# A planned decoder layer on one core: other buffers for the end of the last batch, the true length of one fp32 matmul in the planner, and new dates

## The chip, the core and the metric

The kernel runs on one core of a Trainium2 chip. A core has five engines that run side by side, each through its own instructions in order: TensorE (PE, matrix products into the accumulators in PSUM), VectorE (DVE), ScalarE (ACT), GpSimd (POOL) and SyncE (SP, which here issues nearly all DMA transfers). They wait for each other by semaphores alone. The metric is the device time of one execution in microseconds (us). Before the change the runs took 1061.47, 1062.81 and 1063.2 us (median 1062.81).

## The reference

One decoder layer over 8 batches of 512 rows of width 256, in fp32, with a layer norm after each of three parts:

```python
# 1: linear attention in chunks of 32 rows, gated
S = einsum('bncd,bnkd->bnck', Qc, Kc) * mask        # decay ** distance, causal
out = sigmoid(x @ W_g.T) * (S @ V) @ W_o.T + x
x = layernorm(x + out)
# 2: cross-attention, 16 heads of 64, over 512 context rows
qw, kw, vw = x @ Wq + bq, ctx @ Wk + bk, ctx @ Wv + bv
a = softmax(where(key_mask, qw @ kw.T / 8, -inf))
x = layernorm(x + (a @ vw) @ Wo + bo)
# 3: FFN with ternary weights, hidden size 1024, and a path of rank 16
h = bitlinear(x, w_fc) + gate * (x @ v.T @ fast_b.T @ u.T)
x = layernorm(x + bitlinear(relu(h) ** 2, w_proj))
```

`bitlinear` rounds a weight row to -1, 0 or 1 by its mean magnitude and scales it with that mean.

## The kernel before

**Arithmetic.** Nearly every fp32 product is made of two fp16 parts, a high one and a low one (`x - high`), and of three products of them (`PASSES`). So wherever a matrix is made, ACT (or POOL) writes the high part and DVE or POOL the low one. The ternary weights need no low part.

**Units.** Batch after batch, the cross-attention goes over 8 pairs of heads, and for each pair over 4 blocks of 128 query rows: 256 units in all, `(b, p, qt)`. One unit is: 6 score matmuls of 64 by 512 on PE, two heads side by side on the two halves of the array (`scores`, tile `s`); for each head a row maximum on DVE that also adds the mask (`tensor_tensor_reduce`, in the trace CUSTOM_DVE and a read of the accumulator, tile `nm`); for each head an exponential on ACT (tile `e`); the high part of the probabilities on ACT or POOL and the low part on DVE (`split_p`, tile `ph`); a DMA transpose of two units together on SP's queue (`pT` from `ph`, in the last two head pairs one unit at a time, the very last by PE); and 24 small matmuls of 64 columns (`attend`, tile `av`) some six units later. After four units of a pair the division, the split and a transpose give `oT` (through `of` and `oh`; in the last two pairs after two units, through `ofl` and `ohl`, with PE transposes).

**Between the units** stand the other stages, cut into pieces: k, v, q of head pairs to come (tiles `pk`, `pvv`, `pq`, `W`), the linear attention of the next batch (`gen_l0`), and the output projection (`pwo`) and FFN (`ph`, `r`, `rh`, `py`, `y`) of the batch before. In batch 0 the weights are prepared there too (`setup_wo`, `setup_ffn`). After the last unit there is a written tail: the rest of the projection of batch 7 (`wo_tail`, tile `pwl`) and its FFN in two halves of 256 rows (`ffn_tail`: `pz`, `r4`, `rhl`, `pyl`, `yl`), row blocks one at a time.

**The planner sets the order.** The body of the kernel only records operations. Each carries a date, `nc.prio`: the number of the unit at which it is recorded, plus an offset by its kind (`LATE`; `TP` in the tail). How early a piece of a stage is recorded is set by the budget that is pulled from its queue at each unit (`PULL`: "k" for k, q and v, "l" for the next batch's first part, "w" for the weights, "f" for projection and FFN, "g" the same in batch 7). `schedule` then runs a model of the engines, with a length for each operation from `cost`, and at each moment starts on every free engine the ready operation of the earliest date; `REACH` says how much later a date it may take in place of an earlier one that would collide with POOL. What comes out is one fixed order for each engine. All instructions are emitted from one line, 451, so the profile tells them apart by tile names.

**Buffers are part of the plan.** A tile with a tag takes a slot of a ring; most rings are served in the order in which the program recorded the tiles (`in_order`), and a tile that has no slot holds back its operation in the plan. The rings that matter here: `tmp2` (4 slots of 2 KB: `of`, `r4`, `y`, and before the change `ofl`, `ohl`, `yl`), `t4` (5 slots: `rh`, and before the change `rhl`), `pT` and `ph` (3 slots each, probabilities), `x1T` and `ctxh` (2 each: the inputs of q and of k and v).

**The fp32 matmul.** One product is left in fp32: in `setup_ffn`, `ones` times `dg` spreads the scale of the second FFN weight over all partitions (tile `ps2`, shown as `ps`), and DVE copies it to `s2b`. `cost` gave every matmul `n / 2400 + 0.0025` us for n columns.

Of the kernel before, what the change touches and what calls it, by code (L numbers as in the profile page):

```python
# [11 lines left out]
F16 = mybir.dt.float16  # L12
F32 = mybir.dt.float32
# [5 lines left out]
B, T, D = 8, 512, 256  # L19
H, DH = 16, 64  # L20
# [6 lines left out]
LAG = 4  # L27
BURST = 2
MARGIN = 0.0
REACH = 9.52  # L30
SPARE = 1
DLATE = 1.6
PTS = 3
PHS = 3
NWP = 4
TP = (0.35, 0.96, 1.15, 3.0, 0.5, 5.1)
STICK = 2.09
HOLD = 0.18
HIGH = ("apaa", "paaa", "papp")
LATE = {"k": 0.0, "q": 0.0, "v": 0.53, "w": -0.33, "l": -0.41, "o": -0.91, "f": 0.31, "s": 0.0, "a": 0.91, "t": 0.0, "x": 0.31, "e": 0.0, "c": -1.28, "d": -0.95}  # L40
PULL = {"k": 5.13, "l": 2.62, "w": 3.61, "f": 4.71, "g": 5.48}

PASSES = ((0, 0), (0, 1), (1, 0))

# [109 lines left out]
class Recorder:  # L154
# [34 lines left out]
    def add(self, engine, method, args, kw):  # L189
# [9 lines left out]
        if engine in ("DVE", "ACT") and method[:3] != "dma" and self.prio >= 0:  # L199
            src = ins[0].t if ins else None  # L200
            if method == "tensor_tensor_reduce":
                o.prio += LATE["t"]
            elif method == "activation" and args[2] == AF.Exp:
                o.prio += LATE["x"]
            elif src is not None and src.pool[:2] == "ps":
# [45 lines left out]
    def cost(self, o, ins, outs):  # L251

        n = max([int(np.prod(x.shape[1:])) for x in outs + ins] or [0]) if o.engine != "PE" else outs[0].idx.size
        psum = any(x.t.pool[:2] == "ps" for x in ins + outs)
        ones = sum(x.idx.size == 1 and x.t.free > 0 for x in ins)
        o.half, o.port = None, o.engine == "POOL"
        o.dma = o.method[:3] == "dma"
        if o.dma:
            x = (outs or ins)[0]
            if o.method == "dma_start_transpose":  # L260
                blocks = n / 128
                o.occ, o.lat = 0.1 * blocks + 0.4, 0.115 * blocks + 0.55
            else:
                size = {F32: 4, F16: 2}.get(x.t.dt, 1)
                o.occ, o.lat = 0.45, n * size * x.shape[0] / (380e3 if self.prio < 0 else 210e3) + (1.2 if size == 1 else 0.1)
        elif o.engine == "PE":
            o.occ = n / 2400 + 0.0025
            o.lat = o.occ + 0.17
            if ins[0].p1 - ins[0].p0 == 64:
                o.half = ins[0].p0  # L270
        elif o.engine == "DVE":
            lat = 0.145 + n * 1.042e-3
            if o.method == "tensor_tensor_reduce":
                o.occ, o.lat = 0.615, 0.8
                return
            if not psum and o.method in ("tensor_copy", "tensor_scalar") and n >= 512:
                lat = 0.12 + n * 0.62e-3
            if psum and ones and o.method == "scalar_tensor_tensor":
                lat += 0.065
            if n <= 8:  # L280
                lat = 0.19 if o.method == "reciprocal" else 0.175 if o.method == "bn_aggr" else 0.145
            o.occ, o.lat = lat - 0.085, lat
            o.port = not psum and o.method in ("tensor_tensor", "scalar_tensor_tensor", "tensor_scalar", "tensor_copy")
        elif o.engine == "ACT":
            lat = 0.165 + n * 0.83e-3 + (0.0 if psum else 0.04) + 0.07 * ones
            o.occ, o.lat = (lat + 0.01, lat + 0.12) if "accum_out" in o.kw else (lat - 0.11, lat)
        elif o.engine == "POOL":
            if o.method == "tensor_tensor":
                lat = 0.3 + n * 1.67e-3 if n <= 512 else 0.2 + n * 1.9e-3
                if o.args[3] == ALU.pow:  # L290
                    lat = 0.42 + 0.16 * n
            else:
                lat = 0.13 + n * 0.9e-3 if n > 512 else 0.92 if n == 256 and o.kw == {} and o.method == "tensor_scalar" and o.args[-1] == ALU.is_lt else 0.62 if n > 256 else 0.56 if n > 8 else 0.22 + n * 5e-3
            o.occ, o.lat = lat - 0.03, lat


    def schedule(self):
# [37 lines left out]
        while done < len(ops):  # L335
# [10 lines left out]
            while again:  # L346
                again = False
                for e in engines:
# [22 lines left out]
                    while e != "PE" and avail[e]:  # L371
                        x = heapq.heappop(avail[e])
                        if pick is not None and x[0] > pick[0] + REACH:
                            aside.append(x)
# [98 lines left out]
def decoder_kernel(ctx: ExitStack, tc: tile.TileContext, ins: dict, out: bass.AP):  # L473
# [4 lines left out]
    wk = ctx.enter_context(Pool(nc, "wk", 1))  # L478
# [5 lines left out]
    def t4(name, shape, dt=F16):  # L484
        return wk.tile(shape, dt, tag="t4", name=name, bufs=5)

    def tmp2(name, shape, dt=F32):
        return wk.tile(shape, dt, tag="tmp2", name=name, bufs=4)
# [252 lines left out]
    rows, x1T, x2T, ctxh, mb, oT = {}, {}, {}, {}, {}, {}  # L741
# [288 lines left out]
    def ffn_tail(b, i, base, step_):  # L1030
        row = rows[b]
        rh, py = {}, {}
        ts = slice(256 * i, 256 * i + 256)
        PL = 3
        for s_ in range(8 + PL):
            nc.prio = base + step_ * s_
            if s_ == 0:
                zst = ffn_z(b, ts, f"{b}_{i}", ("zst", "sph")[i])
            if s_ < 8:
                j = s_  # L1040
                r4 = ffn_h(b, j, ts, zst, f"{b}_{i}", True)
                hl = t4(f"rhl{i}{j}", [128, 2, 256])
                if i == 0 or j % 2:
                    nc.scalar.activation(r4, r4, AF.Square)
                else:
                    nc.vector.tensor_tensor(r4, r4, r4, ALU.mult)
                if j % 2:
                    nc.scalar.copy(hl[:, 0], r4)
                else:
                    nc.vector.tensor_copy(hl[:, 0], r4)  # L1050
                (nc.vector if j % 3 == 2 or (i == 1 and j == 7) else nc.gpsimd).tensor_tensor(hl[:, 1], r4, hl[:, 0], ALU.subtract)
                rh[j] = hl
            if s_ >= PL:
                j = s_ - PL
                if j == 0:
                    for t in range(2):
                        py[t] = misc(f"pyl{i}{t}")[:, :D]
                hl = rh.pop(j)
                for t in range(2):
                    for a in range(2):  # L1060
                        nc.tensor.matmul(py[t], hl[:, a, t * 128:(t + 1) * 128], tpj[:, j, :],
                                         start=(j == 0 and a == 0), stop=(j == 7 and a == 1))
            yield
        for t in range(2):
            tt = 2 * i + t
            y = tmp2(f"yl{tt}", [128, D])
            nc.vector.tensor_tensor(y, py[t], s2b, ALU.mult)
            nc.vector.tensor_tensor(row[:, tt], row[:, tt], y, ALU.add)
            layernorm(b, row, EPS, "c", tt, 1, True)
            nc.sync.dma_start(out[b, tt * 128:(tt + 1) * 128], row[:, tt, :])  # L1070
        yield


    pT, av, den = {}, {}, {}
# [58 lines left out]
    def attend(u):  # L1133
        b, p, qt = u
# [3 lines left out]
        o, v, t = av[b, p][:, qt], vp[b, p], pT.pop(u)  # L1138
# [7 lines left out]
        if tail:  # L1146
            if qt == 0:
                oT[b, p] = wk.tile([128, 2, T], F16, tag="oT", name=f"oT{b}_{p}", bufs=8)
            if qt % 2:
                d = den[b, p][:, qt - 1:qt + 1, :]  # L1150
                nc.vector.reciprocal(d, d)
                of = tmp2(f"ofl{p}{qt}", [128, 2, 2, DH])
                nc.vector.scalar_tensor_tensor(of, av[b, p][:, qt - 1:qt + 1], sc, d.unsqueeze(3).broadcast_to([128, 2, 2, DH]), ALU.mult, ALU.mult)
                oh = tmp2(f"ohl{p}{qt}", [128, 2, 2, 128], F16)
                ofv = of.rearrange("p t h n -> p t (h n)")
                nc.scalar.copy(oh[:, 0], ofv)
                nc.vector.tensor_tensor(oh[:, 1], ofv, oh[:, 0], ALU.subtract)
                dst = oT[b, p][:, :, (qt - 1) * 128:(qt + 1) * 128].rearrange("p a (t n) -> p a t n", t=2)
                for a in range(2):
                    pe_T(dst[:, a], [oh[:, a, t_] for t_ in range(2)], f"o{p}{qt}{a}", a)  # L1160
            return
        if qt == 3:
            d = den.pop((b, p)).rearrange("p t h -> p (t h)")
            nc.vector.reciprocal(d, d)
            of = tmp2(f"of{b}_{p}", [128, 4, 128])
# [3 lines left out]
            oh = wk.tile([128, 2, 4, 128], F16, tag="oh", name=f"oh{b}_{p}", bufs=1)  # L1169
# [62 lines left out]
    for p in range(2):  # L1232
        g = gen_kv(0, p)
# [13 lines left out]
    def at(i, off):  # L1247
        now[0], nc.prio = i, i + off
# [18 lines left out]
    for i, u in enumerate(units):  # L1267
        b, p, qt = u
# [26 lines left out]
        f = 1 + (0.5 - p % 2) * 0.2  # L1295
# [18 lines left out]
    U = len(units)  # L1314
# [18 lines left out]
            if pend:  # L1333
                attend(pend.pop(0))

    at(U, 1)
    bf.drain()
    at(U, TP[0])
    rest(len(pend) - 4)
    wo_tail(0)  # L1340
    f0, f1 = ffn_tail(b, 0, U + TP[1], TP[2]), ffn_tail(b, 1, U + TP[3], TP[4])
    go(f0, 3)
# [10 lines left out]
    go(f0, 1)  # L1353
    at(U, TP[5])
    ffn_end(b - 1)
# [47 lines left out]
```

## Time and profile before

The profiled execution took 1061.94 us; its span, from the first to the last instruction, is 1060.1 us.

| | busy us | share of the span |
|---|---|---|
| PE matmul | 998.2 | 94% |
| DVE | 986.9 | 93% |
| ACT | 879.4 | 83% |
| POOL | 544.8 | 51% |
| packets of SP's queue | | 95.6% of 16 DMA engines |

The largest groups: exponentials (512 of 705 ns on ACT), row maxima (512 of 710 ns on DVE), low parts of the probabilities (256 of 1298 ns on DVE), `av` (6144 matmuls), scores (1536 matmuls), and 131 transposes of `ph` on SP's queue, 7.5 us from issue to landing in the median.

How to read it: start times are us from the span's start. The first unit's row maximum starts at 45.4, that of batch 1 at 168.1, of batch 2 at 284.4, of batch 7 at 898.3; the middle batches take 122 to 123 us each. In a timeline a row gives start, length, engine, line, operation, tiles and shapes, and how many instructions it merges; in square brackets stands the idle time of the engine before it and what ended that. In the table of stretches each engine has its busy time and, after x, its instructions; PEclk is the mean TensorE clock that was granted, 1.00 being full. The share of a busy engine is no proof that it is the bound: a row can hold time in which the instruction only waited for a port or a pipeline.

### The profile page before, as it was taken

To read this page: it belongs to the slowest core of one execution; us is meant where nothing else is said; L and a number is where in the kernel's file an instruction comes from. 1 tells how busy PE (TensorE), PEld (TensorE's weight loads), DVE (VectorE), ACT (ScalarE), POOL (GpSimd) and SP (SyncE) were. 2 spreads that over 40 slices of the span, in tenths; PEclk is the share of its full clock that TensorE was granted. 3 is DMA by queue.
4 is the path that set the end of the run, shared out by engine and by line. 5 is a ranking of instruction groups with operands and counts; after the bars stand their busy time and mean duration, and the time that the engine had idled before them with its cause. 6 is when DMAs were issued, how large, how long until landed. Compare 5 with 4: busy or idle time off the path is not lost.

```text
span 1060.1 us, 29949 instructions
## 1 busy us (share of the span) xinstructions
PE 998.2 (94%) x11976; PEld 639.3 (60%) x11976; DVE 986.9 (93%) x2101; ACT 879.4 (83%) x1876; POOL 544.8 (51%) x513
## 2 busy tenths in 40 slices
PE   7986889999999999999999999999999999999986
PEld 4644545665666656665666656766567656665664
DVE  7999989999999989999899989999899998998976
ACT  7787778889977998789977898879977889878836
POOL 0251282256841596245861577426962548443635
PEclk9999989999999999999999999999999999999989
DMA  8289799999999999989999999999999999999861
GB/s 306 99 147 186 133 214 186 164 180 191 186 185 189 174 179 168 207 155 189 185 184 204 162 185 179 192 189 156 195 163 214 154 185 170 187 167 201 138 115 41
DMA packets 646636, 185.65 MB, mean 175 GB/s; under 512 B 628448, under 2 KB 641376, under 8 KB 646496
## 3 DMA queue, kind: packets, MB, share of 16 engines
q1 hardware_dynamic: 645632, 183.42, 95.6%
q8 instruction: 93, 1.52, 0.6%
q10 hardware_dynamic: 864, 0.32, 0.1%
q14 instruction: 47, 0.39, 0.1%
HBM read 21.18 MB, written 4.19 MB: 24 GB/s over the span
## 4 chain that ended last, share of the span: by engine, by line
PE 41%; ACT 17%; DVE 17%; DMA 12%; issue 6%; POOL 4%; SPq 2%; ACTq 0%; POOLq 0%; DVEq 0%
PE av L451 8%; PE s L451 8%; DMA pT<-ph 6%; ACT e L451 6%; DVE s L451 5%; DVE ph L451 5%; PE pk L451 4%; PE pq L451 4%; PE pwo L451 4%; ACT r L451 4%; PE py L451 3%; PE pvv L451 3%; ACT ph L451 3%; SPq L451 2%; DVE W L451 2%
## 5 line engine op out<-in xcount | busy, mean ns | idle before, releaser
L451 ACT ACTIVATE e<-s,nm 128x512 f32<-128x512 f32 x512 | 354.4, 705 | 100.7 <-DVE nm L451 83.3
L451 DVE SCALAR_TENSOR_TENSOR ph<-e,ph 128x1024 f16<-128x1024 f32 x256 | 330.6, 1298 | 27.6 <-ACT ph L451 25.2
L451 DVE CUSTOM_DVE_ANT_0 s<-s,mb 128x512 f32<-128x512 f32 x512 | 342.3, 710 | 6.1 <-PE s L451 4.5
L451 PEld LDWEIGHTS <-pT 128*128 128x128 f16 x6144 | 198.7, 99 | 59.5 <-issue 29.5
L451 PE MATMUL av<-v,pT 128*128 128x64 f16 x6144 | 213.2, 194 | 12.4 <-DMA pT<-ph 12.2
L451 PE MATMUL s<-W 64*128 64x512 f16 x1536 | 205.6, 379 | 12.5 <-ACT e L451 10.8
L451 ACT ACTIVATE ph<-e 128x1024 f16<-128x1024 f32 x186 | 200.0, 1081 | 2.4 <-DMA pT<-ph 0.3
L451 POOL TENSOR_SCALAR ph<-e 128x1024 f16<-128x1024 f32 x70 | 84.8, 1211 | 227.3 <-ACT e L451 214.7
L451 PEld LDWEIGHTS <-W 64*128 64x128 f16 x1536 | 64.2, 94 | 110.4 <-issue 59.4
L451 PEld LDWEIGHTS <-wqkv 128*128 128x128 f16 x768 | 70.3, 98 | 82.6 <-issue 18.0
L451 POOL TENSOR_TENSOR oh<-of,oh 128x512 f16<-128x512 f32 x62 | 86.6, 1396 | 65.0 <-ACT oh L451 63.1
L451 ACT ACTIVATION_READ_ACCUMULATOR e<-s,nm 128x1 f32 x512 | 113.5, 222 | 0.0
L451 PE MATMUL pk<-ctxh,wqkv 128*128 128x512 f16 x384 | 103.0, 382 | 6.2 <-POOL ctxh L451 6.1
L451 PE MATMUL pvv<-wqkv,ctxh 128*128 128x256 f16 x768 | 102.0, 274 | 0.3 <-DVE v L451 0.3
L451 POOL TENSOR_TENSOR rh<-r,rh 128x512 f16<-128x512 f32 x56 | 75.1, 1345 | 52.4 <-ACT rh L451 52.4
L451 PE MATMUL pq<-x1T,wqkv 128*128 128x512 f16 x384 | 97.2, 380 | 0.5 <-DVE bob L451 0.3
L451 PEld LDWEIGHTS <-ctxh 128*128 128x128 f16 x768 | 71.4, 98 | 26.1 <-issue 13.0
L451 PEld LDWEIGHTS <-oT 128*128 128x128 f16 x768 | 73.8, 100 | 20.8 <-issue 5.3
L451 PE MATMUL pwo<-wo,oT 128*128 128x256 f16 x672 | 84.2, 276 | 0.4 <-ACT e L451 0.4
L451 DVE DVE_READ_ACCUMULATOR2_ANT nm<- 128x1 f32 x512 | 72.4, 141 | 0.0
L451 PE MATMUL ph<-x2T,tfc 128*128 128x512 f16 (+1 forms) x288 | 68.4, 356 | 0.3 <-ACT r L451 0.3
L451 PE MATMUL py<-tpj,rh 128*128 128x256 f16 x448 | 58.4, 273 | 0.0
(190 smaller groups left out, 1492.4 us busy)
## 6 DMA issues: line engine op xcount, KB each, us to landing
row<-in_x SPq DMA_DIRECT2D x8, 512.0 KB, 5.4
xs<-in_xT SPq DMA_DIRECT2D x7, 512.0 KB, 4.9
ctxs<-in_ctxT SPq DMA_DIRECT2D x7, 512.0 KB, 4.5
out_dram<-row SPq DMA_DIRECT2D x7, 512.0 KB, 3.6
wqs<-in_wqkv SPq DMA_DIRECT2D x6, 512.0 KB, 7.2
pT<-ph SPq DMA_TRANSPOSE x131, 7.5
wos<-in_wo SPq DMA_DIRECT2D x4, 256.0 KB, 2.8
fcs<-in_w_fc SPq DMA_DIRECT2D x2, 512.0 KB, 4.9
```

What stands on the lines that cost most here:

```text
L451: getattr(real[x.engine], x.method)(*[r(a) for a in x.args], **{k: r(a) for k, a in x.kw.items()})
```

## The change

Three edits. The buffers of the last batch's end: `rhl` of each half of `ffn_tail` becomes one tile of all eight parts, in a slot of the ring `pT` (first half) or `ph` (second half) in place of eight slots of `t4`; `yl` and `ofl` go from `tmp2` to the ring `x1T`, `ohl` to the ring `ctxh`. The planner's length of a matmul whose operand isn't fp16 becomes n / 200 us. And the dates: `REACH`, three of the six old entries of `TP` and a new seventh, two entries each of `PULL` ("k", "g") and `LATE` ("w", and "t", the row maxima, 0.55 of a unit earlier).

```diff
-REACH = 9.52
+REACH = 9.66
...
-TP = (0.35, 0.96, 1.15, 3.0, 0.5, 5.1)
+TP = (0.0, 2.0, 0.8, 3.0, 0.5, 5.1, 2.0)
...
-LATE = {"k": 0.0, "q": 0.0, "v": 0.53, "w": -0.33, "l": -0.41, "o": -0.91, "f": 0.31, "s": 0.0, "a": 0.91, "t": 0.0, "x": 0.31, "e": 0.0, "c": -1.28, "d": -0.95}
-PULL = {"k": 5.13, "l": 2.62, "w": 3.61, "f": 4.71, "g": 5.48}
+LATE = {"k": 0.0, "q": 0.0, "v": 0.53, "w": -0.48, "l": -0.41, "o": -0.91, "f": 0.31, "s": 0.0, "a": 0.91, "t": -0.55, "x": 0.31, "e": 0.0, "c": -1.28, "d": -0.95}
+PULL = {"k": 4.41, "l": 2.62, "w": 3.61, "f": 4.71, "g": 4.5}
...
         elif o.engine == "PE":
-            o.occ = n / 2400 + 0.0025
+            o.occ = n / 2400 + 0.0025 if ins[0].t.dt is F16 else n / 200
             o.lat = o.occ + 0.17
...
+        rhl = wk.tile([128, 8, 2, 256], F16, tag=("pT", "ph")[i], name=f"rhl{i}", bufs=(PTS, PHS)[i])
...
-                hl = t4(f"rhl{i}{j}", [128, 2, 256])
+                hl = rhl[:, j]
...
-            y = tmp2(f"yl{tt}", [128, D])
+            y = wk.tile([128, D], F32, tag="x1T", name=f"yl{tt}", bufs=2)
...
-                of = tmp2(f"ofl{p}{qt}", [128, 2, 2, DH])
+                of = wk.tile([128, 2, 2, DH], F32, tag="x1T", name=f"ofl{p}{qt}", bufs=2)
...
-                oh = tmp2(f"ohl{p}{qt}", [128, 2, 2, 128], F16)
+                oh = wk.tile([128, 2, 2, 128], F16, tag="ctxh", name=f"ohl{p}{qt}", bufs=2)
...
-    at(U, 1)
+    at(U, TP[6])
     bf.drain()
     at(U, TP[0])
```

Every date enters the plan of the whole kernel, so the order of all engines differs from batch 0 on. The instructions themselves are the same, engine by engine.

## The prediction

> **What bounds the kernel now.** I read first the busy shares of the page, then the busy time by stretches of 10 to 40 us, then the timelines of single engines in the few places where DVE idles, last the groups by line and shape.
>
> ```profile
> PE 998.2 (94%) x11976; PEld 639.3 (60%) x11976; DVE 986.9 (93%) x2101; ACT 879.4 (83%) x1876; POOL 544.8 (51%) x513
> q1 hardware_dynamic: 645632, 183.42, 95.6%
> ```
>
> No engine is the bound alone: PE, DVE and the transposes on SP's queue are all over 90% busy, ACT 83%. A change of order that adds no instruction can then gain only what is lost in stretches where one of them waits. The stretches show where that is:
>
> ```profile
> core 0: us, PE busy (x) PEld busy (x) DVE busy (x) ACT busy (x) POOL busy (x), PEclk, DMA share, GB/s
> 100.00:110.00 10.00, 7.85 (x84) 5.24 (x81) 8.39 (x17) 4.97 (x9) 0.00 (x0) 0.83 1.11 217
> 280.00:320.00 40.00, 40.00 (x526) 27.39 (x523) 39.79 (x88) 32.42 (x71) 20.98 (x19) 1.00 1.04 192
> 969.00:988.00 19.00, 19.00 (x232) 11.25 (x230) 15.93 (x28) 18.97 (x41) 10.83 (x9) 1.00 0.80 140
> 1005.90:1031.50 25.60, 21.10 (x308) 16.18 (x303) 18.88 (x44) 9.14 (x23) 9.83 (x11) 0.87 0.75 130
> ```
>
> The middle (280 to 320) is full. Batch 0 (100 to 110) has holes on all engines. In batch 7 ACT is full from 969 to 988, with the FFN of batch 6 beside the softmax, and DVE idles 3 us. From 1006 on nothing is full: the end is a chain of short steps. The single waits:
>
> ```profile
> 97.79 0.15 DVE L451 TENSOR_SCALAR sp<-sp 128x1 f32<-128x1 f32 x1 [0.78 <-ACT abpj L451]
> 102.96 1.20 PE L451 MATMUL ps<-dg,ones 128*128 128x256 f32 x2 [2.15 <-DVE dg L451]
> 103.95 2.65 PE L451 MATMUL av<-v,pT 128*128 128x64 f16 x48
> 104.19 0.42 DVE L451 COPY s2b<-ps 128x256 f32<-128x256 f32 x1 [0.71 <-PE ps L451]
> 980.61 1.23 SPq L451 DMA_TRANSPOSE oT<-oh  x1
> 987.76 10.10 SPq L451 DMA_TRANSPOSE pT<-ph  x2
> 997.95 2.14 SPq L451 DMA_TRANSPOSE oT<-oh  x1
> 1000.20 14.09 SPq L451 DMA_TRANSPOSE pT<-ph  x5
> 1015.68 5.46 SPq L451 DMA_TRANSPOSE pT<-ph  x2
> 984.45 3.25 DVE L451 SCALAR_TENSOR_TENSOR ph<-e,ph 128x1024 f16<-128x1024 f32 x2
> 1016.30 0.42 DVE L451 SCALAR_TENSOR_TENSOR ofl<-av,den 128x256 f32<-128x256 f32 x1 [3.14 <-PE av L451]
> 1016.64 1.22 DVE L451 SCALAR_TENSOR_TENSOR ph<-e,ph 128x1024 f16<-128x1024 f32 x1
> ```
>
> The fp32 matmul keeps PE idle for 2.15 us, and DVE then waits for it. SP's queue is empty from 981.84 to 987.76, until DVE's ph ends at 987.70; from there transpose follows transpose to 1021.14. One of the last ph of DVE (1016.64) stands behind an ofl that waits 3.14 us.
>
> **The change part by part.** Both programs hold the same instructions on every engine (2101 on DVE); only order and buffers differ, so each price is a wait that goes or comes. I laid the two orders side by side and summed, between the row maxima of chosen units, the median time of each instruction of DVE and ACT by its group; for PE, matmuls at the shortest rows of a full stretch, from one group's start to the next's (six of 512 columns 1.29, sixteen of 256 1.75, 48 of 64 1.41, six score matmuls 0.75 and twelve 1.40). Sums are "before to after".
>
> *fp32 matmul.* Its planned length goes from 0.11 to 1.28 us; the row says 1.20 for the pair of records. In the new order PE has six pq (1.29) and 12 av (0.35) between the scores and this matmul, which fills 1.64 of the 2.15 us; on DVE the copy s2b stands behind both row maxima and a ph (1.14) and no longer waits. Gone: 0.71 on DVE; the 0.78 for abpj also stands behind both maxima now and can go. DVE's work from the first unit of batch 0 to that of batch 1 goes from 113.3 to 114.4, in batch 1 from 109.4 to 108.6: 0.3 more up to there. Bounds: +0.3 (DVE there waits for something else, rows of 0.8 to 0.9 for scores and for a load are next) and -2.6 (both waits, and the 1.1 us that the 48 av took above the usual 1.5). I take -1.4, the two DVE waits, as DVE is the fullest there.
>
> The granted clock is weighed here. The row: 2.15 us of idle PE, then 0.83 as the mean clock of 100 to 110 and 2.65 us for 48 av. The Trainium skill ("TensorE: Matmul & The Clock Gate", Part 1) ties the half clock to an idle window of about 3.4 us; by it this gap would cost no clock, and filling it would win 0 of that 1.1 us on PE. The trace speaks against the rule as a threshold for one gap, but DVE is the bound in that stretch, so my -1.4 is the same by either.
>
> *Dates, REACH, PULL in batches 1 to 6.* From batch 2 to batch 7 DVE's sum is 566.4 in both and ACT's 516.2, PE's 584.3 to 579.5, in 614.0 us. Within a batch they shift: from head pair 1 to 3 of batch 4 (32.2 us) PE's sum, the largest there, goes from 33.7 to 37.6; from pair 5 to 7 (34.6 us) from 35.5 to 33.6 (ACT's from 33.6 to 33.2). A loss of 3.9 stands against a gain of 1.9 in each batch; neither need come, since PE can work ahead of the scores (its 33.7 took 32.2). The score matmuls form 168 groups in place of 186; six alone take 0.75 and twelve together 1.40, so each merge spares 0.10, 1.8 in all; PE is 41% of the chain: -0.7. Bounds over five batches: -9.5 (only the 1.9 counts) and +10 (3.9 less 1.9). I take -0.7, nearer to the sums over whole batches, which are equal on DVE and ACT.
>
> *Batch 7 up to its last scores.* The FFN of batch 6 is pulled at 4.5 a step in place of 5.48, which the new buffers permit: ofl and ohl were in the ring of four (tmp2) that serves in program order, with the y of batch 6 ahead of them, and rhl in the ring that held rh of batch 6. Now y60 and y62 can stand behind them. From pair 4 to the third unit of pair 7 (953.4 to 1006.8, 53.4 us) the largest sum goes from PE's 48.4 to ACT's 44.7 (-3.7) and DVE's from 44.1 to 41.2 (-2.9); from pair 0 to 4, in 55.1 us, DVE's, the largest, goes from 54.6 to 54.2. With the smaller of the first two that is -3.3. It reaches the end only if SP's queue starts earlier: the ph that ended its hole has 2.5 us less work before it on DVE, 7.4 less on ACT. Bounds: -5.9, the whole hole, and 0, if the queue starts as before. I take -3.3.
>
> *The end.* 50 matmuls of batch 6's py now stand behind the last scores: PE's sum from there to the first pz goes from 15.9 to 20.8 in 25.6 us. What hides the 4.9 is PE's waits there (21.10 busy of 25.60, at a clock of 0.87); without that cover they cost 4.9. On DVE the ph of 1016.64 now stands ahead of that ofl, so the 3.14 are no longer before it; but its transpose comes after others on SP's queue, which was full until then, so what is late next is the queue, and little of the 3.14 counts. New in the way: y62 (0.68) ahead of the copy to x2T, and on POOL row6 += y62 (1.43 at 1012.84) ahead of rstdb of row block 2, of which mvb's own lateness hides about half: 0.6 and 0.7. The steps from the first pz on are the same, and rhl, yl in other buffers cost nothing: no wait of the end was on their slots. Bounds: -3.1 (the whole wait) and +4.9 (py uncovered). I take -0.4: half of the 3.14 against 1.3, rounded down.
>
> The sum: -1.4 - 0.7 - 3.3 - 0.4 = -5.8. The profiled execution took 1061.94 (span 1060.1 and 1.8 around it), 0.87 under the median of the runs; against its own time that is 1056.1, and on the median 1062.81 it is **1057.0**.
>
> **The rivals.** *A: PE sets the pace in pairs 1 to 3 of each middle batch* (slower than before). For it: PE's 33.7 there lasted 32.2, so PE was already the pace; against it: the PE work is only moved, and PE was ahead elsewhere. Its price is 3.9 - 1.9 = 2.0 a batch, +10 over five, with the other three parts (-5.1): 1067.7. It decides from a net 1.0 a batch (5.1 / 5). *B: the middle gains.* PE absorbs the heavier stretch and the relief of pairs 5 to 7 stays: -1.9 a batch, -9.5; for it speak DVE's waits for ACT's ph in these batches, 21.6 us in ten waits; against it that ACT's sum of two pairs falls by only 0.4. With -5.1: 1048.2. *C: the end does not move*, so the change does not do there what it says: the transposes are serial for 33 us, and if their queue starts as before, the relief of ACT at 969 to 988 is waited away behind it. Then -1.4 - 0.7 remain: 1060.7.
>
> **How the numbers follow.** My forecast has 0.45, A 0.22, B 0.13, C 0.20. The runs of before spread by 1.7 us, so 0.2% (2.1 us, 1060.7 to 1064.9) is about what can be told from no change. Faster: 0.42 of the forecast, B whole, half of C less a little (0.09): 0.64. Same: 0.03 of the forecast, the rest of C, none of A: 0.14. Slower: A, 0.22. The range goes down to where about half of B is inside and up to where about half of A is (a net of 1.8 a batch): 1049.5 to 1066.7. The forecast's own range, both signs being open, is 1053 to 1061.
>
> **What would show it.** In the profile after: the fp32 matmul with a wait under 1 us and s2b without one, and no dip of the clock at 100 to 110; from pair 1 to 3 in a middle batch 32 to 33 us (36 would be A); the hole in SP's queue before the two transposes of pair 5 of batch 7 under 3 us; the last ph of DVE not behind a wait; the first pz 3 to 6 us earlier than 1031.53, and about 28.6 us from there to the end, as now. Wrong it would be, above all, through the middle: one microsecond a batch there weighs as much as all that I found at both ends.

## The result, and the profile after

The changed kernel takes 1067.55 us in the median of five runs (1066.53 to 1069.05), the kernel before in the same comparison 1063.04 us. The ratio is 1.0047, with a 95% interval of 1.0036 to 1.0059. It is slower by half a per cent; I had forecast 1057.0 us and given "slower" 0.22. The time, 1067.7, that I gave to rival A was met almost exactly, but not in the place that A names.

The profiled execution took 1067.55 us, with a span of 1065.7. The busy line and the queue line of the page:

```profile
PE 999.4 (94%) x11976; PEld 638.5 (60%) x11976; DVE 989.4 (93%) x2101; ACT 880.8 (83%) x1876; POOL 554.9 (52%) x513
q1 hardware_dynamic: 645632, 183.42, 94.9%
```

All shares are within a point of those before, with 5.6 us more of span, and the instructions are the same: over the whole kernel the loss is waiting, not work. Where it lies is read best from the start of the row maximum of chosen units, in us from the start of each span:

| stretch | before | after | difference | forecast |
|---|---|---|---|---|
| start to first unit of batch 1 | 168.1 | 175.6 | +7.4 | -1.4 |
| batches 1 to 6 | 730.2 | 735.8 | +5.7 | -0.7 |
| batch 7 to the third unit of pair 7 | 108.5 | 99.8 | -8.7 | -3.3 |
| from there to the end | 53.3 | 54.5 | +1.2 | -0.4 |
| span | 1060.1 | 1065.7 | +5.6 | -5.8 |

Of the 5.7, batch 1 has 2.9 and each of the batches 2 to 6 about 0.6. The stretches of the profile after (engine by engine busy time and instructions, then PEclk, DMA share and GB/s, as in the prediction):

```profile
110.00:130.00 20.00, 16.04 (x171) 9.50 (x170) 14.46 (x31) 11.93 (x26) 5.21 (x4) 0.83 1.02 168
290.00:330.00 40.00, 39.43 (x505) 25.68 (x502) 39.65 (x85) 33.98 (x73) 20.36 (x19) 1.00 1.08 191
960.00:980.00 20.00, 19.02 (x237) 10.30 (x231) 20.00 (x45) 17.85 (x39) 12.14 (x11) 1.00 1.05 178
991.70:1015.70 24.00, 23.55 (x310) 14.98 (x307) 22.16 (x47) 23.84 (x55) 17.76 (x14) 1.00 1.19 195
1010.00:1030.50 20.50, 18.98 (x323) 16.67 (x324) 17.94 (x36) 10.72 (x25) 11.64 (x10) 1.00 1.08 187
```

The middle is full as it was. Batch 7 is fuller: DVE no longer idles at 960 to 980, and the clock of the end is 1.00 where it was 0.87. A hole is now at 110 to 130, where DVE, the fullest engine of batch 0, is busy 14.46 of 20 us and PE runs at 0.83 of its clock. The single rows, from the timelines of the engines:

```profile
106.68 4.86 SPq L451 DMA_TRANSPOSE pT<-ph  x1
107.88 0.70 PE L451 MATMUL ps<-dg,ones 128*128 128x256 f32 x2
110.13 0.42 DVE L451 COPY s2b<-ps 128x256 f32<-128x256 f32 x1
111.63 1.46 SPq L451 DMA_TRANSPOSE tpj<-pjt  x1
113.14 1.48 SPq L451 DMA_DIRECT2D sv<-in_vT  x1
114.72 0.42 SPq L451 DMA_DIRECT2D ur<-in_u  x1
115.35 1.20 PE L451 MATMUL av<-v,pT 128*128 128x64 f16 x32 [2.20 <-DMA pT<-ph]
116.34 0.23 ACT L451 ACTIVATE vst<-sv 128x32 f16<-128x32 f32 x1 [5.22 <-DMA sv<-in_vT]
116.48 0.67 ACT L451 ACTIVATE e<-s,nm 128x512 f32<-128x512 f32 x1
116.61 0.19 DVE L451 SCALAR_TENSOR_TENSOR vst<-sv,vst 128x32 f16<-128x32 f32 x1 [2.29 <-ACT vst L451]
118.16 1.02 PE L451 MATMUL pu<-identh,uh 128*16 128x128 f16 x8 [1.61 <-ACT uh L451]
982.07 11.19 SPq L451 DMA_TRANSPOSE pT<-ph  x2
1023.21 1.21 DVE L451 SCALAR_TENSOR_TENSOR ph<-e,ph 128x1024 f16<-128x1024 f32 x1
1037.13 0.60 PE L451 MATMUL pz<-x2T,vst 128*128 128x256 f16 x4
```

The fp32 matmul (107.88) and its copy no longer wait. But a few us later ACT stands for 5.22 us, until the small matrix vT has landed: its load is behind two transposes on SP's queue, and the exponential of a unit stands behind its conversion `vst` on ACT. DVE waits behind ACT, PE behind `uh`, which is made from the load right after (`u`). In the kernel before the same loads also stood behind a `pT` and the `tpj`, but were issued 4.8 us earlier:

```profile
108.30 0.53 SPq L451 DMA_DIRECT2D sv<-in_vT  x1
111.25 0.22 ACT L451 ACTIVATE vst<-sv 128x32 f16<-128x32 f32 x1
112.87 0.54 DVE L451 TENSOR_TENSOR ur<-ur,rs 128x128 f32<-128x128 f32 x1 [0.82 <-DMA ur<-in_u]
```

There ACT came to `vst` 2.95 us after the load's issue and found it landed. After the change ACT comes to it at about the same time (111.1), which is 2.0 us before the load is issued. The Trainium skill ("TensorE: Matmul & The Clock Gate", in the section on the architectural detail of the array) calls ACT's and DVE's queues strictly first in, first out; the `e` at 116.48 agrees: it ran only behind the 5.22 us, though DVE had read out its row maximum at 113.67.

This is not the first place of batch 0 that is late. The stretch from its first unit to the first unit of pair 2, before and then after:

```profile
45.40:66.00 20.60, 18.69 (x166) 10.01 (x165) 20.60 (x51) 19.82 (x50) 8.62 (x9) 1.00 0.55 102
```

```profile
44.90:71.40 26.50, 23.18 (x198) 12.48 (x196) 26.50 (x59) 20.34 (x50) 13.64 (x11) 0.94 0.60 113
```

DVE is busy all the time in both, and the new order has put 4.3 us more of its work there, by the median lengths (a low part of the probabilities, two `v`, a `W` and three `fct`). So 5.9 us are lost before either load is issued. From pair 2 to 4 0.4 us come back, though DVE has 2.9 us less to do there; pair 4, with the loads, takes 4.2 us longer than before, and the rest of the batch 1.8 less: together 8.0 us from the first unit of batch 0 to that of batch 1. (The first unit itself starts 0.5 us earlier, hence the 7.4 of the table.)

### The profile page after: what moved, and what is told of

It reads as the page before. It is cut to its first block, busy times and chain, and to the rows that moved or that the text cites. A ratio compares the mean times of both kernels' runs of the same rounds, so it can differ in the third digit from the quotient of the medians.

```text
span 1065.7 us, 29915 instructions
## 1 busy us (share of the span) xinstructions
PE 999.4 (94%) x11976; PEld 638.5 (60%) x11976; DVE 989.4 (93%) x2101; ACT 880.8 (83%) x1876; POOL 554.9 (52%) x513
## 4 chain that ended last, share of the span: by engine, by line
PE 43%; DVE 20%; ACT 18%; DMA 12%; issue 5%; POOL 2%; SPq 0%; ACTq 0%; POOLq 0%; DVEq 0%
DMA pT<-ph 9%; PE av L451 8%; PE s L451 8%; PE pwo L451 7%; ACT e L451 6%; DVE ph L451 5%; DVE s L451 5%; ACT r L451 4%; PE pvv L451 3%; PE pk L451 3%; PE pq L451 3%; ACT ph L451 2%; PE py L451 2%; ACT rh L451 2%; PE pg L451 2%
## 5 line engine op out<-in xcount | busy, mean ns | idle before, releaser
L451 DVE SCALAR_TENSOR_TENSOR ph<-e,ph 128x1024 f16<-128x1024 f32 x256 | 334.1, 1310 | 28.1 <-ACT ph L451 26.2
L451 PE MATMUL s<-W 64*128 64x512 f16 x1536 | 208.5, 381 | 19.2 <-ACT e L451 14.6
L451 POOL TENSOR_SCALAR ph<-e 128x1024 f16<-128x1024 f32 x70 | 95.7, 1368 | 248.1 <-ACT e L451 224.7
L451 POOL TENSOR_TENSOR oh<-of,oh 128x512 f16<-128x512 f32 x62 | 91.4, 1474 | 91.3 <-ACT oh L451 90.2
L451 PE MATMUL pk<-ctxh,wqkv 128*128 128x512 f16 x384 | 100.0, 383 | 4.5 <-POOL ctxh L451 3.0
L451 PE MATMUL pvv<-wqkv,ctxh 128*128 128x256 f16 x768 | 96.0, 274 | 0.2 <-ACT e L451 0.2
L451 POOL TENSOR_TENSOR rh<-r,rh 128x512 f16<-128x512 f32 x56 | 84.1, 1511 | 18.2 <-ACT rh L451 15.4
L451 PEld LDWEIGHTS <-ctxh 128*128 128x128 f16 x768 | 73.7, 98 | 19.6 <-issue 7.6
```

Source lines behind the costliest of these rows:

```text
L451: getattr(real[x.engine], x.method)(*[r(a) for a in x.args], **{k: r(a) for k, a in x.kw.items()})
```

## The experiments

Theories at the outset. Theory 1: two separate effects, a loss made in batches 0 and 1 by an early date or by the length of the fp32 matmul (1k: PULL "k"; 1t: LATE "t"; 1f: the length), and a gain in batch 7 made by the buffers with PULL "g". Rivals: that the two are coupled, so that batch 7 only wins back what was put off; and A of the prediction, that the middle makes the loss. Ratios are against the kernel before on the same chip, with 95% intervals; medians from different comparisons are from different chips. Starts and stretches are from one profiled execution of each kernel. Where that execution lies far from the median of its kernel's runs, the starts show where time goes rather than how much: it is 2.3 us below for the end alone, 4.6 above for "k" alone, 2.4 above for the old "w", 2.0 above for vT's load alone and 2.7 to 3.0 below for the buffers with TP and for the first two kernels of the last part of this section.

### The change in two halves

The end alone: the kernel before with the three buffer edits and

```diff
-TP = (0.35, 0.96, 1.15, 3.0, 0.5, 5.1)
+TP = (0.0, 2.0, 0.8, 3.0, 0.5, 5.1, 2.0)
-PULL "g": 5.48
+PULL "g": 4.5
```

> The kernel before with only the parts that reach batch 7 and the end: the buffer edits, PULL "g" at 4.5 and the new TP. Theory 1 (two separate effects: the loss of the changed kernel is made in batches 0 and 1 by a date, the gain in batch 7 by the buffers with "g"): the first unit of batch 7 starts as in the kernel before, within 0.5 us, and all 7.5 us that batch 7 and the end won in the changed kernel are won here too: 1054 to 1057 us, ratio about 0.993. Rival (coupled: batch 7 wins only what the earlier batches had put off, so it has less to win when they are as before): 1059 to 1062 us. Rival A of the prediction says nothing of this kernel beyond its other parts: about 1059.

The rest alone:

```diff
-REACH = 9.52
+REACH = 9.66
-LATE "w": -0.33, "t": 0.0
+LATE "w": -0.48, "t": -0.55
-PULL "k": 5.13
+PULL "k": 4.41
-            o.occ = n / 2400 + 0.0025
+            o.occ = n / 2400 + 0.0025 if ins[0].t.dt is F16 else n / 200
```

> The kernel before with only the other parts: REACH, LATE "w" and "t", PULL "k", and the length of the fp32 matmul. Theory 1 (two separate effects): the first unit of batch 1 comes about 7 us late and that of batch 7 about 13 us late, as in the changed kernel, and the end is not better than before: 1072 to 1077 us. Rival (coupled): batch 7 gives back a good part of it without the buffers: 1066 to 1070. Rival A (the middle is the place of the loss): batches 2 to 6 lose 2 us each; Theory 1 says 0.6 or less each.

The end alone took 1060.92 us (0.9988, interval 0.9975 to 1.0001), the rest alone 1070.23 (1.0071, 1.0044 to 1.0099). So the early dates and the length make the loss: batch 1 starts 7.4 us late and batch 7 13.0 us late, as in the changed kernel, and batches 2 to 6 lose 2.1 us together, which speaks against A. But neither theory holds whole. From the first unit of batch 7 to the end, the end alone won 4.4 us in its profiled execution (0.9 in the medians of the whole time), and the early dates alone, without any buffer, won 5.2. Up to the third unit of pair 7 the shares are 4.6 and 3.4, together nearly the 8.7 of the changed kernel. That batch 7 wins back work that had been done ahead is excluded: the work started before its first unit, summed with the median length of each kind of instruction, differs by 0.4 us or less on DVE, ACT and POOL.

### One date at a time

```diff
-PULL "k": 5.13
+PULL "k": 4.41
```

> The kernel before with PULL "k" at 4.41 alone. Theory 1k (the slower pull of k, q and v makes the loss of batch 0, since these stages then come later and beside the preparation of the weights): batch 1 starts 5 to 8 us late, 1070 to 1073 us. Theory 1t (the earlier row maxima make it) and theory 1f (the fp32 length makes it): within 3 us of before, 1060 to 1066.

```diff
-LATE "t": 0.0
+LATE "t": -0.55
```

> The kernel before with LATE "t" at -0.55 alone: the row maxima on DVE are planned half a unit earlier, so the other work of DVE in batch 0 is put behind them. Theory 1t: batch 1 starts 5 to 8 us late and the middle batches lose 0.5 each, 1070 to 1075 us. Theory 1k and theory 1f: within 3 us of before, 1060 to 1066.

They took 1081.63 (1.0173, 1.0145 to 1.0202) and 1093.72 us (1.0292, 1.0264 to 1.0321): each of the two dates alone is far worse than all the early edits together. Batch 1 starts 13.3 and 9.4 us late, and the batches 2 to 6 lose 2.1 and 4.8 us each, where the changed kernel loses 0.6. Theories 1k and 1t each took the other for harmless; both dates hurt, and most of the harm in the middle cancels. The first part of batch 0 is made by "k" more than by "t": from its first unit to that of pair 2 it takes 27.1 us with "k" alone and 22.9 with "t" alone (before 20.6, with all edits 26.5). In batch 0 the timelines of both, first of "k" and then of "t", have the same two rows on ACT:

```profile
100.53 1.06 ACT L451 ACTIVATE abpj<-pjs 128x1024 f16<-128x1024 f32 x1 [4.40 <-DMA pjs<-in_w_proj]
109.73 0.23 ACT L451 ACTIVATE vst<-sv 128x32 f16<-128x32 f32 x1 [6.71 <-DMA sv<-in_vT]
```

```profile
98.19 1.06 ACT L451 ACTIVATE abpj<-pjs 128x1024 f16<-128x1024 f32 x1 [4.06 <-DMA pjs<-in_w_proj]
107.06 0.23 ACT L451 ACTIVATE vst<-sv 128x32 f16<-128x32 f32 x1 [6.38 <-DMA sv<-in_vT]
```

ACT waits for loads of weights, for vT as in the changed kernel and, worse than there (1.30 us), for the second half of `w_proj`.

### The length of the fp32 matmul, and "w"

The length alone in the kernel before, and the changed kernel with the old length:

```diff
-            o.occ = n / 2400 + 0.0025
+            o.occ = n / 2400 + 0.0025 if ins[0].t.dt is F16 else n / 200
```

> The kernel before with the true length of the fp32 matmul alone. The prediction's term says 1.4 us faster (bounds 0.3 slower and 2.6 faster), all of it won before the first unit of batch 1. Theory 1 says no more than 1.5 us either way there, 1060 to 1064. Theory 1f says 5 to 8 us slower, 1066 to 1070.

> The changed kernel with the old length of the fp32 matmul in the planner. The two orders differ in 14 places of DVE, all in batch 0. By the term of the prediction (the true length takes away two waits of DVE, 1.4 us) this kernel is 1.4 us slower than the changed one: about 1069. By theory 1f (the length is what lengthened batch 0) it is 5 to 8 us faster: 1060 to 1062. By theory 1 it is within 1.5 us of the changed kernel: 1066 to 1069.

Alone it took 1065.93 us (1.0025, 1.0010 to 1.0040), so it costs 1.1 to 4.3 us where I had -1.4. Two rows of its timelines show that the wait I had counted on is still there, and another is longer:

```profile
103.99 0.67 PE L451 MATMUL ps<-dg,ones 128*128 128x256 f32 x2 [2.15 <-DVE dg L451]
114.08 0.29 DVE L451 TENSOR_TENSOR ur<-ur,rs 128x128 f32<-128x128 f32 x1 [1.99 <-DMA ur<-in_u]
```

PE waits for `dg` as before, 2.15 us; only the wait of `s2b` is gone, and DVE waits 1.99 us for `u` in place of 0.82. The changed kernel with the old length took 1067.06 us (1.0039, 1.0024 to 1.0053), no different from the changed one, and its fp32 matmul doesn't wait either. So in the new order the length neither took that wait away nor made the loss: the other dates did the first, and 1f falls.

The changed kernel with LATE "w" as before:

```diff
-LATE "w": -0.48
+LATE "w": -0.33
```

> The changed kernel with LATE "w" (the preparation of the weights in batch 0) at -0.33 again. If w makes the loss of batch 0, its first unit of batch 1 starts 5 us or more earlier and the time is 1060 to 1063 us. If k and t make it (theory 1k, 1t), batch 1 still starts 6 us or more late, and the time is 1065 to 1070.

It took 1071.83 us (1.0082, 1.0051 to 1.0112): "w" is no cause. By the medians the new "w" repairs some of what "k" and "t" break, but the interval meets that of the changed kernel (1.0036 to 1.0059). ACT's wait for vT is 5.07 us here.

### The old dates in batch 0 only

```diff
+        first = b < 1
+        LATE["t"] = 0.0 if first else -0.55
+        LATE["w"] = -0.33 if first else -0.48
+        PULL["k"] = 5.13 if first else 4.41
```

> The changed kernel with the three early dates as before (LATE "t" 0.0 and "w" -0.33, PULL "k" 5.13) while batch 0 is recorded, the new ones from batch 1 on, and the old length of the fp32 matmul. Theory 1 (the loss is made by the new dates beside the preparation of the weights): the first unit of batch 1 starts within 1.5 us of the kernel before, batch 7 within 4 us, and the end is 1056 to 1060 us. Rival (coupled: work that one date puts off must be done in the next batch, so old dates in batch 0 only move the loss to the hand-over): batch 1 loses 5 us or more instead, 1064 to 1069 us.

It took 1065.73 us (1.0024, 1.0008 to 1.0040). Batch 0 is that of the kernel before, without a wait for vT, and batch 1 starts 0.6 us late. `REACH` stayed new in this run, so beside the old dates it makes no loss in batch 0; alone it was not tried. Batch 1 then loses 4.4 us, batch 2 3.2 and the next four 4.5, so that batch 7 starts 12.8 us late, as late as in the changed kernel. Theory 1 said 4 us at most; of its terms only that on batch 1's start held. The time is in the range of the rival, which had the loss move to the hand-over. The new dates cost something in the batches that follow too (0.6 a batch in the changed kernel), and more right behind the change from one set to the other.

### The loads themselves

Here nothing is planned anew; the planned order is kept, and loads are moved on SP's queue afterwards. First the load of vT, in its own buffer, as early as the last user of that buffer allows:

```diff
         self.schedule()
+        for name in ["sv", "ur"]:
+            ...   # o = its load, i = its place, older = what it depends on or what held its slot
+            j = max(self.ops.index(x) for x in older) + 1
+            self.ops.insert(j, self.ops.pop(i))
```

> The changed kernel with nothing moved but two loads on SP's queue, after planning: that of vT goes ahead of a transpose pT and one of tpj (from 113.14 to about 107), that of u ahead of nothing but comes right behind tpj. In the changed kernel ACT stands idle for 5.22 us at 116.34 until vT has landed, and DVE behind it for 2.29 us. If this wait is part of the loss of batch 0 (theory 1, its mechanism: work in a fixed order behind a load that was issued late), head pair 5 of batch 0 starts 2 to 5 us earlier than in the changed kernel, batch 1 2 to 4 us earlier, and the time is 1063 to 1066 us. If batch 0 is bound elsewhere (DVE's own work or PE's clock): within 1 us of the changed kernel, 1066.5 to 1068.5.

It took 1066.99 us (1.0043, 1.0026 to 1.0060), no gain. From its timelines:

```profile
106.98 0.53 SPq L457 DMA_DIRECT2D sv<-in_vT  x1
111.38 0.21 ACT L457 ACTIVATE vst<-sv 128x32 f16<-128x32 f32 x1
114.01 0.53 SPq L457 DMA_DIRECT2D ur<-in_u  x1
117.67 0.29 DVE L457 TENSOR_TENSOR ur<-ur,rs 128x128 f32<-128x128 f32 x1 [2.79 <-DMA ur<-in_u]
```

ACT's 5.22 us are gone, and DVE waits 2.79 us for the next load of the chain, which was as late as ever. One wait had hidden the other, though the two were not all: PE waits 2.78 us for a transpose here (2.20 in the changed kernel). So both loads were given buffers of their own and issued before batch 0, in the changed kernel and in the kernel before:

```diff
         self.schedule()
+        loads = {x.args[0].t.name: x for x in self.ops if x.method == "dma_start" and isinstance(x.args[0], View)}
+        for name in ("sv", "ur"):
+            o = loads[name]
+            o.bufs[0].slots, o.bufs[0].pool = None, "cst"
+            self.ops.remove(o)
+            self.ops.insert(self.ops.index(loads["fb"]) + 1, o)
```

> The changed kernel in its planned order, but vT and u have buffers of their own and their two loads are issued on SP's queue behind those of gate and fast_b, before batch 0. No engine can wait for them at 110 to 118 then. If the two late loads make the loss of pairs 4 and 5 of batch 0: head pair 5 starts 3 to 5 us earlier than in the changed kernel and the time is 1062.5 to 1065. If the transposes pT (PE waits 2.2 to 2.8 us for one at 115 to 116 in both runs) and PE's clock make it: pair 5 starts at most 1.5 us earlier, and the time is 1065.5 to 1067.5.

> The kernel before in its planned order, with the same two loads ahead of batch 0. Its waits for them are 0.82 us on DVE, 1.16 on PE and 1.30 on ACT. If they count in full, about 1 us faster: 1060.5 to 1062. If not, equal: 1062 to 1063.

The changed kernel with early loads took 1059.23 us: 0.9979 of the kernel before (0.9967 to 0.9990), against 1.0047 without them. The kernel before with early loads took 1060.44 (0.9993, 0.9983 to 1.0003). Two loads of 16 and 64 KB were worth 0.68% in the one order and 0.07% in the other, and with them out of the way the change is not a loss: 1059.23 against 1060.44 on the same chip. The stretch from 110 to 130 again, in the changed kernel with early loads:

```profile
110.00:130.00 20.00, 17.12 (x218) 10.49 (x217) 17.70 (x37) 15.34 (x33) 5.34 (x4) 1.00 0.98 165
```

DVE is busy 17.70 us in place of 14.46, and PE has its full clock. Head pair 5 of batch 0 starts 3.9 us earlier than in the changed kernel, as expected: pair 4 takes 17.9 us, in the kernel before 17.5, in the changed one 21.6. The move does two things that these runs don't separate. No engine waits for the loads, and SP's queue is free of them: the two transposes behind them are issued at 112.11 in place of 115.27. PE's 2.20 us of wait for a transpose that is issued at 106.7 and 106.6 are gone too, and nothing here shows why. The time fell by more than 3.9 us. In the two profiled executions batch 1 starts 3.1 us earlier, batch 7 5.7 and the end comes 7.9 earlier. What lies behind batch 0 comes in steps of 2 us and less, at places where the order is the same in both; executions of one order differ by as much there (from the last scores to the end the run with vT's load alone moved took 52.4 us and the changed kernel, in the same order, 50.0). I don't read causes out of those steps.

What remains: against the kernel before with early loads, from the first unit on, the changed order with early loads still loses 8.3 us up to batch 7, 4.8 of them in batch 0, and batch 7 and the end win 9.1. A third late load is the second half of `w_proj`, for which ACT still waited 1.84 us at 102. It was moved ahead of five transposes, to 83.37:

```diff
+        o = loads["pjs1"]
+        ...
+        self.ops.insert(self.ops.index(older[-1]) + 1, self.ops.pop(i))   # older: what held its slot
```

> As the run of the changed kernel with vT and u loaded early, and also the second load of w_proj is issued as early as its buffer allows: behind the last use of the weights that lie in it, ahead of two transposes tfc, two of pT and one of tpj (from about 97 to 84). If a late load in this stretch costs what waits for it, ACT's wait of 1.84 us and DVE's of 1.16 behind it go and head pair 4 of batch 0 starts 1 to 2 us earlier: 1057 to 1058.5 us. If these waits lie beside other work: 1059 to 1060, or slower if the load now delays the transposes behind it.

It took 1059.54 us (0.9955, 0.9940 to 0.9970). The intervals of this and of the run without this move (0.9967 to 0.9990) overlap, on two chips, and the medians in us are alike; the profiled executions have the same span, 1057.8 us, with pair 4 of batch 0 0.4 us earlier. From its timelines:

```profile
83.37 0.36 SPq L461 DMA_DIRECT2D pjs<-in_w_proj  x1
```

The wait for `w_proj` is gone, and ACT waits 1.73 us for PE at 96.53, where it had waited 1.12. So a late load need not cost its wait: by the profile this one lay beside other work, though the ratios leave room for a gain. The other 4 us of batch 0 are there by pair 2, before any of these loads: with the loads early too, the stretch to its first unit takes 26.5 us in place of 20.6, with DVE full. Why the later pairs, with less of DVE's work, don't win them back is open. What I can name there, unproved: in the profile after PE is idle for 6.22 us at 85.11 and has 0.57 of its clock from 82 to 90.

### The end, part by part

The buffers alone, the buffers with "g", and the buffers with TP, each in the kernel before:

```diff
+        rhl = wk.tile([128, 8, 2, 256], F16, tag=("pT", "ph")[i], name=f"rhl{i}", bufs=(PTS, PHS)[i])
...
+            y = wk.tile([128, D], F32, tag="x1T", name=f"yl{tt}", bufs=2)
...
+                of = wk.tile([128, 2, 2, DH], F32, tag="x1T", name=f"ofl{p}{qt}", bufs=2)
...
+                oh = wk.tile([128, 2, 2, 128], F16, tag="ctxh", name=f"ohl{p}{qt}", bufs=2)
```

> The kernel before with the buffer edits alone (rhl, yl, ofl, ohl in other rings). The prediction held that the buffers only permit the later pull g and that no wait of the end was on their slots; then ofl (3.14 us of wait on DVE) and ohl are served earlier or later by nothing but the plan: within 1.5 us of before, 1060.5 to 1063.5. Rival (the buffers are the gain): 2 us or more faster, 1057 to 1060.

> The kernel before with the buffer edits and PULL "g" at 4.5, without the new TP. The run with TP too gained 8 us on the kernel before up to the first unit of pair 6 of batch 7, gave 5 of them back up to the last scores, and ended 1.3 us faster in the medians. If g alone makes that first gain and the giving back (less FFN work beside the softmax of pairs 4 and 5, more beside the last two pairs, where ACT has no idle time left), this run shows both, and ends within 1.5 us of that run: 1059.5 to 1062.5. If TP makes the giving back (the rest of batch 6 set later at the end): 1055 to 1058.

> The kernel before with the buffer edits and the new TP, with PULL "g" at 5.48 as before. By the prediction's terms batch 7 keeps its pace up to the last scores (no 3.3 won there), and the end moves by -0.4 (bounds -3.1 and +4.9): 1061 to 1063 us. If the gain of the changed kernel's end, 2.1 us from the last scores, comes from TP and the buffers and not from g: 1058 to 1060.5.

They took 1062.83 (0.9999, 0.9984 to 1.0014), 1061.45 (0.9987, 0.9972 to 1.0001) and 1063.09 us (1.0003, 0.9988 to 1.0017). The buffers alone show no gain (the interval is 1.5 us to both sides), as the prediction held. With "g" the first unit of pair 6 of batch 7 comes 7.9 us earlier, counted from the start of batch 7, and most is given back by the last scores (1.0 us are left); so "g" makes both, and TP neither. The stretch from pair 6 to the last scores, in the kernel before and in the run of the end alone:

```profile
987.60:1008.00 20.40, 20.40 (x281) 15.02 (x278) 20.40 (x44) 15.84 (x38) 13.62 (x11) 1.00 1.10 175
```

```profile
980.90:1006.60 25.70, 23.40 (x326) 15.00 (x323) 22.92 (x45) 23.83 (x55) 20.55 (x15) 1.00 1.20 185
```

ACT's busy time goes from 15.84 to 23.83 us: the FFN work put off from pairs 4 and 5 stands here, where DVE and PE had been full, and now they wait.

### A version that beats both

The end of the change in the kernel before, with the two loads early; then the same with "g" at 5.0; then that with the load of `w_proj` early too.

```diff
-PULL "g": 4.5
+PULL "g": 5.0
```

> The kernel before with the buffer edits, PULL "g" and TP of the change, and the two loads ahead of batch 0. If the gains add up (0.12% for the first three, up to 1 us for the loads): 1059 to 1061 us, a ratio of 0.997 to 0.999. If the loads are worth nothing: 1061, 0.9988.

> As the run before, with PULL "g" at 5.0, between the old value and the new one. At 4.5 batch 7 gained 8 us up to pair 6 and gave 5 back in the last two pairs, where ACT had 0.2 us of idle time in 24. If half of the work put off fits there without filling ACT, less is given back than half: 1057 to 1060 us. If gain and loss scale alike: 1060 to 1062.

> The fastest version so far (the kernel before with the buffer edits, the new TP, PULL "g" at 5.0, and vT and u loaded early: 0.9968) with the second load of w_proj ahead of two transposes tfc and one of pT. In the kernel before ACT and DVE wait 0.78 us for that half: 0 to 0.8 us faster, a ratio of 0.996 to 0.997.

They took 1059.61 (0.9980, 0.9965 to 0.9994), 1059.19 (0.9968, 0.9953 to 0.9983) and 1057.75 us (0.9945, 0.9924 to 0.9966). At 5.0 the stretch from pair 6 to the last scores is

```profile
981.90:1004.00 22.10, 21.26 (x296) 14.35 (x295) 21.10 (x44) 18.25 (x42) 14.38 (x10) 1.00 0.97 154
```

with ACT at 18.25 us and less given back. All three beat the kernel before, and so the changed one; between them the intervals overlap. The step from the second to the third (0.23%) is as large as that from the changed kernel with two early loads to that with three (0.24%), between the same two chips and with profiles that don't show it (spans 1054.7 and 1055.2), so it may lie in the comparison and not in the load. Early dates for batch 7 alone, where they won 5.2 us, were not tried.

## Why the prediction was wrong, step by step

**The fp32 matmul and batch 0 (-1.4; came +7.4): the step that failed.** The two waits add to 1.5, and their removal was to be the whole of batch 0. The signs that I named all came: no wait of the matmul, none of `s2b`, no dip of the clock at 100 to 110. They were no proof. First, the wait was taken away by the other dates and not by the length. Second, the bound of +0.3 rested on "rows of 0.8 to 0.9 for scores and for a load are next": I took the length of the next wait from the old order. In the new one SP's queue issues the load of vT 4.8 us later and ACT comes to `vst` no later than before; where the longest wait for these loads had been 0.82 us (DVE for `u`), ACT now waits 5.22 for vT, with 2.29 on DVE behind it and 1.61 on PE. With the loads early all but 0.4 of the 4.2 us that pair 4 had lost are won. Laying the orders side by side showed this place; I summed work there and didn't ask when each load would be issued and who would stand behind its user. Third, I gave the dates no price in batch 0 at all: my sums of DVE's work went from the first unit of a batch to that of the next (113.3 to 114.4) and hid that 4.3 us more of it stand before pair 2, where DVE has no idle time; that stretch became 5.9 us longer. What keeps the later pairs from winning this back stays open.

**Batches 1 to 6 (-0.7; came +5.7).** Inside the bounds of -9.5 and +10. The sums of work over batches 2 to 6, equal in both orders, were right, and the loss there is small (0.6 a batch). Pairs 1 to 3 of batch 4 took 32.0 us, before 32.2, as I said; 36 would have been A. The price was made of five batches, 2 to 6; half of the 5.7 is batch 1, which I had priced by its work alone, with 0.8 less on DVE. What makes its 2.9 is open; with the loads early 1.7 are left.

**Batch 7 to the third unit of pair 7 (-3.3; came -8.7).** The mechanism was right: SP's queue is full now, its gap before the two transposes of pair 5 (982.07) is 0.1 us. The early dates alone keep a gap of 4.7 us before a transpose (at 997.29); with the buffers and "g" it is 0.2, and batch 7 wins 3.0 up to the third unit of pair 7, with TP too 4.6. The bound of -5.9, the whole hole, was wrong, since the early dates shorten this stretch by 3.4 as well, which I didn't consider.

**The end (-0.4; came +1.2).** Inside the bounds. (Half of 3.14 against 1.3 is -0.3, not -0.4.) The last `ph` of DVE (1023.21) has no wait before it, and from the first `pz` (1037.13) to the end there are 28.6 us, as said. `pz` came 5.6 us later than before, not 3 to 6 earlier; counted from the third unit of pair 7 it is 1.2 later. What I missed is the row 991.70:1015.70: ACT busy 23.84 of 24.00, which takes the last scores 3.3 us further.

**The clock.** The row weighed there (2.15 us of idle PE, then half clock) can now be set beside others. With the length alone, the same 2.15 us again come before a low clock (0.60 as the mean of 104 to 108). With vT's load moved, 2.78 us of idle PE at 116.30 come before 32 `av` in 1.11 us, the pace of the 28 in 0.98 us at 109.90 in the kernel before, where the clock was full; with vT's load moved the half clock comes only from 118.9 to 122.3, after 1.01 us more of idle. In the kernel before and with the length alone the gap was not the only one: 1.65 and 1.61 us of idle stand just before, and PE was busy 1.31 and 1.25 of the 3.4 us ahead of the half clock. But with vT's load moved it was busy 1.51 of 3.4 us (112.0 to 115.4) and kept its clock at first. So the length of one gap doesn't tell when the half clock comes: neither 2.15 against 2.78 us here, nor the about 3.4 us of the Trainium skill ("TensorE: Matmul & The Clock Gate", Part 1), read as the length of one gap, which is longer than each of these gaps. That DVE was the bound and the clock worth nothing in -1.4 stays untested.

## What to carry to other kernels

Where a plan is made anew, a wait that goes need not say anything about the time. Look in the new order for each late transfer with a fixed place in a queue, and ask which engine reaches its user first and what stands behind that user. And compare the work up to each step inside a batch, not only from batch to batch: here 4.3 us more of DVE's work stood in a stretch where DVE was full, the stretch took 5.9 us longer, and most of that was not won back in the batch. Two small loads behind transposes were worth 0.68% in one order and 0.07% in another: here it paid to put loads that depend on nothing ahead of the busy part, in buffers of their own. Dates that were chosen together can't be priced one by one: two of them alone cost 1.7% and 2.9%, all the early edits together 0.7%.

## What the runs showed that I had not expected

- A date of half a unit for the row maxima costs 32 us alone; with all the other early edits beside it the cost is 8.
- Taking away the longest wait of a stretch (5.22 us) gained nothing, taking away the next one as well gained 7 us.
- PE's clock changed with the two loads: 0.83 in the changed kernel at 110 to 130, 1.00 with them early in the same order. The half clock of the changed kernel comes right behind PE's 2.20 us of wait for a transpose (mean 1.00 from 112.8 to 116.2, then 0.50 to 123.0), so it is not shown that the waits for the loads made it.
